# Attended features times W as seven block products instead of eight, with a new order of the work

## The chip, the cores and the metric

One core of a Trainium2 chip. The metric is the device time of one execution in microseconds (us), as the median of several runs; the kernel before takes 2569.77 us (three runs, 2566.48 to 2571.89).

## What is computed

The input is 128 graphs of 128 nodes with 256 features (`x`, fp32), an integer adjacency per graph and a node mask (all ones here). Three graph-attention layers run first, then a gated graph network with three steps; each layer is added to its input.

```python
# layers 0, 1, 2: attention
h = relu(layernorm(x));  Wh = h @ W
e = leaky_relu((Wh @ a1)[:, :, None] + (Wh @ a2)[:, None, :], 0.2)
x = x + elu(softmax(where(adj > 0, e, -9e15)) @ Wh)     # times nodemask in layer 2
# layer 3: gated graph network, three steps i
h = relu(layernorm(x))
m = h @ weight[i];  aggr = einsum('bst,bsd->btd', adj != 0, m)
h = gru_cell(aggr, h, w_ih, w_hh, b_ih, b_hh)
x = x + h
```

## The kernel before, in words

**Groups.** The graphs are worked in 33 groups: two graphs in the first and the last, four in the 31 between (`SIZES`). For each group the function `gat` does the three attention layers and the normalization ahead of layer 3, and `gru` the three recurrent steps. A graph has 128 nodes, so a node is a partition, and a group of four is 512 columns (T).

**Attention of one group and layer** (`attention`). VectorE takes statistics (L519), GpSimd the inverse root (L525, L528), ScalarE normalizes into `xn` (L602), VectorE forms the two scores per graph with a multiply and sum into a scratch tile `scr` (L610). ScalarE and VectorE form the softmax in `em`; its transpose goes by DRAM into `at` (`exchanged`, L552 and after). Then come the two products that matter here. `gathered(k)` (L723) multiplies `xn` by the attention: per half k of the features four matmuls of 128 columns (one per graph) into one bank of PSUM, which ScalarE copies to `ah[:, k]` (L730). `pair(j)` (L742) multiplies these attended features by W: for each of two graphs two matmuls (k = 0, 1) of 256 columns, the stationary side being a 128x128 block of `ah`, the moving side the rows k of W. Two graphs fill one bank `hp`. ScalarE takes the exponential of it (L756) and VectorE adds elu to `x` in two instructions (L758, L760). So a call of four graphs has 16 matmuls of 128 columns and 8 of 256.

**Recurrent step** (`gru`). The aggregation (L991) and the gates (L952, L965, L1047). The gates' products are already in the seven-product form: two 2x2 block matrices are multiplied with seven products of blocks instead of eight, for sums of blocks on both sides (`t13`, `t24` of the state and of the aggregate, L929 and L923 on VectorE; the weights' sums made once by `combinations` on GpSimd, L388), and with copies and additions of partial results in PSUM (L1099, L1103, L1106, L1112; L1015, L1017, L1022 for the new state).

**What sets the order.** No instruction is issued where the code stands. `Plan.add` records each instruction with an engine, a cost in us, a rank and the tiles that it reads, writes and takes. `Plan.issue` then walks through all of them, keeping for each engine a time at which it is free, and issues the ready instruction that can start first, or one within `WINDOW` of it with a lower rank; only ranks within `AHEAD` (`EARLY` at the start, until `UNTIL`) of the lowest open one are looked at. `LAG` is the time it allows between a producer on one engine and a consumer on another. Ranks come from `stage(g, l)` and `start(g, i)`: tables `ATT` and `STARTS` for the first groups, lines of slope 3.0 per group after them. The order on each engine is fixed when the kernel is built; on the chip each engine runs its list in order and waits on semaphores. All DMAs are issued by SP.

**Tiles.** PSUM has eight banks: `gat` 2 (both `ahp` and both `hp`, in turn), `gru` 3, `seed` 2, `tr` 1. `scr` has two buffers, `x` six.

Of the kernel before, what the change touches and what calls it, by code (L numbers as in the profile page):

```python
# [14 lines left out]
P = 128  # L15
# [24 lines left out]
class Plan:  # L40
# [4 lines left out]

    LAG = {"PE": 0.26, "DVE": 0.2, "ACT": 0.2, "POOL": 0.15}
    WINDOW = 0.097
    AHEAD = 4.12
    EARLY = 5.00
    UNTIL = -1.46  # L50

# [12 lines left out]
    def add(self, engine, cost, rank, fn, reads=(), writes=(), after=(), takes=()):  # L64
# [4 lines left out]
        vals = list(dict.fromkeys(v for v, _ in reads + writes))  # L69
        vals += [v for v in dict.fromkeys(takes) if v not in vals]  # L70
        op = Op(engine, cost, rank, fn, vals)
        for v in vals:
# [32 lines left out]
    def lag(self, d, engine, data=True):  # L105
        if d.engine == "SP":
            return d.lands
        return 0.0 if d.engine == engine else self.LAG[d.engine] if data else 0.08

# [79 lines left out]
def kernel(  # L189
# [28 lines left out]
    G = 4  # L218
    FAR = 2
    SIZES = [2] + [G] * ((B - 4) // G) + [2]  # L220
    NG = len(SIZES)
# [60 lines left out]

    SETUPS = [-4.77, -3.63, -3.63, -3.63, -3.63, -3.63, -3.63]
    setting = [0]
# [19 lines left out]

    W, VA = [], []

    def attention_weights(l, w, a):
        rank = [-6.42, -7.21, -4.35][l]
        wt, va = const_val(f"w_{l}", [KD, D]), const_val(f"va_{l}", [2, D])
        first = [-11.17, -10.17, -7.80][l]  # L310
        load(256, first, lambda: nc.sync.dma_start(
# [27 lines left out]
        W.append(wt)  # L339
        VA.append(va)  # L340

    for l, (w, a) in enumerate(((w0, a0), (w1, a1), (w2, a2))):
# [4 lines left out]
    def mask():  # L347
        nm = val(su, "nm", [N], "nm")
        nmp = bank("gat", "nmp")
        load(64, setup_rank(), lambda: nc.sync.dma_start(nm.t[:B], nodemask), writes=[nm])  # L350
        add("PE", 0.11, setup_rank(), lambda: nc.tensor.transpose(nmp.t[:, :B], nm.t[:B], ident[:B, :B]),
            reads=[nm], writes=[nmp])
        add("ACT", act(P), setup_rank(), lambda: nc.scalar.copy(nmT.t, nmp.t[:, :B]),
            reads=[nmp], writes=[nmT])
# [183 lines left out]

    def exchanged(srcs, cut, dst, name, n, rank):

# [10 lines left out]
        def blocks(k):  # L551
            add("DVE", dve(n * P), rank, lambda: nc.vector.transpose(  # L552
                tr.t[:, :, :f].rearrange("p j (k b c) -> p k b j c", k=kd, b=n)[:, k],
                cut(k).rearrange("p b (j r) -> p b j r", j=Q),
            ), reads=[srcs[k]], writes=[(tr, k)], takes=[d, dst])
# [13 lines left out]

    def turned_state(src, k, dst, name, n, rank):  # L570

# [7 lines left out]
        ), reads=[(src, k)], writes=[tr], takes=[d, dst])  # L579
        load(64 * n, rank, lambda: nc.sync.dma_start(d.t.rearrange("b p f -> p b f"), tr.t),  # L580
            reads=[tr], writes=[d])

        def back(j):
            load(16 * n, rank, lambda: nc.sync.dma_start(
                dst.t[j * 32 : (j + 1) * 32, : n * P].rearrange("c (m r) -> c m r", r=32),
# [6 lines left out]
    def attention(g, l, xt, cap):  # L592
# [15 lines left out]
        def score(b, s):  # L608
            scr = val(gw, "scr", [D], f"scr_{name}_{b}_{s}")
            add("DVE", dve(D), rank, lambda: nc.vector.scalar_tensor_tensor(  # L610
# [107 lines left out]

        def gathered(k):
            ps = bank("gat", f"ahp_{name}_{k}")  # L720

            def product(b):
                add("PE", pe(P), rank, lambda: nc.tensor.matmul(  # L723
                    summed(ps, b), xn.t[:, b, k * P : (k + 1) * P], turned_weights(b),
                    start=True, stop=True,
                ), reads=[(xn, b), at], writes=[(ps, b)], takes=[ah])

            for b in range(n):
                product(b)
            add("ACT", act(n * P), rank, lambda: nc.scalar.copy(  # L730
                ah.t[:, k, : n * P], ps.t[:, : n * P]), reads=[ps], writes=[(ah, k)])

        for k in range(KD):
            gathered(k)

        def pair(j):
            hp = bank("gat", f"hp_{name}_{j}")
            t = val(gw, "t", [T], f"t_{name}_{j}")

            def product(b, k):  # L740
                c = 2 * j + b
                add("PE", pe(D), rank, lambda: nc.tensor.matmul(  # L742
                    hp.t[:, b * D : (b + 1) * D], ah.t[:, k, c * P : (c + 1) * P],
                    W[l].t[:, k, :], start=(k == 0), stop=(k == KD - 1),
                ), reads=[(ah, k), W[l]], writes=[hp], takes=[t])

            for b in range(2):
                for k in range(KD):
                    product(b, k)
            parts = [(xt, 2 * j), (xt, 2 * j + 1)]  # L750

            def u():
# [8 lines left out]
                u(), t.t, 1.0, u(), op0=OP.min, op1=OP.add), reads=[t, *parts], writes=parts)  # L761

        for j in range(n // 2):
            pair(j)

    def gat(g):
        b0, n = FIRST[g], SIZES[g]
        rank = stage(g, 0)
        xt = val(grp, "x", [G, D], f"x_{g}", bufs=6, cut=n)
        adj_t = val(grp, "adj", [G, N], f"adj_{g}", dtype=I32, cut=n)  # L770
# [57 lines left out]
    def gru(g, xt, am, hn0, h0):  # L828
# [39 lines left out]
        def flat(h):  # L868

            def part(k):  # L870
                add("DVE", 0.42, start(g, 0) - 1.0, lambda: nc.vector.tensor_copy(
                    cut(h.t[:, k, :TG]), first(k)), reads=[h0], writes=[(h, k)], after=[*after, *begun])
# [4 lines left out]
        def step(i, h):  # L877
# [202 lines left out]
            def mixed(c):  # L1080
# [8 lines left out]
                if FAR <= g < NG - FAR:  # L1089
                    ahead.append(state(f"hn{c}", f"hn_{g}_{i + 1}_{c}"))  # L1090
                    turned_state(hnew, c, ahead[c], f"hn_{g}_{i + 1}_{c}", n_g, quick)

# [38 lines left out]
        def end(h):  # L1131
# [3 lines left out]
            if far:  # L1135
                exchanged(
                    [(h, 0), (h, 1)], lambda k: h.t[:, k, :TG].rearrange("p (b j) -> p b j", b=n_g),
                    o, f"o_{g}", n_g, rank,
                )
# [22 lines left out]

    URGENT = 1.00
    SPAN = 2.25
    HEAD = 5.5
    TAIL = 1.5
# [3 lines left out]
    NNR = 0.25  # L1170
    LEAD = 8.5

    ATT = [
        [-8.90, -4.73, -3.23, -1.30],
        [-7.16, -4.64, -3.85, -2.65],
        [-3.70, -1.92, 1.59, 3.59],
        [-0.38, 1.67, 4.29, 4.81],
        [3.81, 5.72, 6.93, 8.03],
        [7.96, 10.27, 13.26, 12.41],
        [9.50, 11.75, 14.74, 15.00],  # L1180
        [12.46, 14.80, 17.00, 18.00],
        [15.66, 17.97, 20.00, 21.29],
        [18.50, 20.75, 23.00, 24.00],
    ]
    STARTS = [
        [1.68, 2.28, 4.42],
        [3.03, 4.63, 6.47],
        [5.97, 6.79, 10.50],
        [9.00, 11.18, 12.82],
        [12.28, 14.00, 16.00],  # L1190
        [14.67, 16.85, 19.17],
        [17.30, 19.87, 22.34],
        [21.00, 23.00, 25.06],
    ]

    def stage(g, l):

        return ATT[g][l] if g < len(ATT) else 3.0 * g - LEAD + (SPAN * l if l < 3 else HEAD)

    def start(g, i):  # L1200

        return STARTS[g][i] if g < len(STARTS) else 3.0 * g + 2.0 * i

# [44 lines left out]
```

## Time and profile before

| | |
|---|---|
| median of 3 runs | 2569.77 us (2566.48 to 2571.89) |
| the profiled execution | 2566.74 us, its span 2565.0 us |
| mean granted TensorE clock | 0.993 |
| L742, features times W | 1536 records of 128x256, 356.2 us busy |
| L723, attention times features | 1536 records of 128x128, 192.5 us busy |
| L610, scores on VectorE | 732 of 128x256, 270.3 us busy |

The profile has records of what each engine did, with start and duration. PE is a TensorE matmul and PEld the load of its stationary side; both are pipelined, so the time of a matmul is the distance from its start to the next one's. DVE is VectorE, ACT ScalarE, POOL GpSimd, SP the engine that issues the DMAs. "Idle before, releaser" is the time for which an engine stood still ahead of an instruction, and whose end let it go on. The chain follows the work that ended last back through whatever released each step.

### The profile page before, as it was taken

Reading aid. Unit: us, or ns where it says so; the run is one execution under the profiler, and the core shown is the slowest. Engines: PE = TensorE matmul, PEld = TensorE weight load, DVE = VectorE, ACT = ScalarE, POOL = GpSimd, SP = SyncE. Lnnn points to the kernel's source line nnn. Section 1 sums busy time; section 2 is a strip of 40 time slices with the busy share of each in tenths; the row PEclk is TensorE's granted clock in tenths of the full one; section 3 lists DMA queues with packets and bytes.
Section 4 is the critical chain, followed back from the end, with each engine's and each line's share of the span. In section 5 each row is a group of like instructions: output and inputs, shape, how many; then the busy total and the mean of one; then the engine's idle time right before and its main releaser. Section 6 shows DMA issues by size and latency. Waiting matters only on the chain.

```text
span 2565.0 us, 39018 instructions
## 1 busy us (share of the span) xinstructions
PE 2527.7 (99%) x12549; PEld 2098.6 (82%) x12549; DVE 2105.9 (82%) x4955; ACT 1768.5 (69%) x4411; POOL 225.1 (9%) x328
## 2 busy tenths in 40 slices
PE   8799999999999999999999999999999999999998
PEld 5688888888888888888888888888888888888887
DVE  6778888888888888888888888888888888888765
ACT  6777676776766776766776666776666777666554
POOL 2210000000000000000000000000000000000000
PEclk8899999999999999999999999999999999999999
DMA  3113343343343333343334333333334443333320
GB/s 106 46 57 97 87 111 108 95 108 95 106 109 99 107 104 95 108 107 103 105 102 96 109 104 106 104 100 100 107 103 104 107 99 101 101 89 97 75 62 13
DMA packets 503123, 245.75 MB, mean 96 GB/s; under 512 B 280579, under 2 KB 472067, under 8 KB 502918
## 3 DMA queue, kind: packets, MB, share of 16 engines
q1 hardware_dynamic: 502918, 243.25, 35.3%
q8 instruction: 100, 1.64, 0.3%
q14 instruction: 105, 0.86, 0.1%
HBM read 139.28 MB, written 103.87 MB: 95 GB/s over the span
## 4 chain that ended last, share of the span: by engine, by line
PE 95%; DVE 2%; ACT 2%; DMA 1%; issue 0%; SPq 0%; POOL 0%; ACTq 0%; DVEq 0%
PE b L965 19%; PE hp L742 13%; PE e L965 13%; PE ni L1047 13%; PE a L965 13%; PE ahp L723 7%; PE agp L991 6%; PE nn L952 6%; PE nnb L952 5%; ACT em L666 0%; DVE scr L610 0%; ACT em L679 0%; PE hnp L852 0%; DMA at<-d_at 0%; ACT hn L791 0%
## 5 line engine op out<-in xcount | busy, mean ns | idle before, releaser
L742 PE MATMUL hp<-w,ah 128*128 128x256 f32 x1536 | 356.2, 384 | 0.5 <-ACT ah L730 0.5
L1047 PE MATMUL ni<-ag,wc_n 128*128 128x512 f32 (+1 forms) x792 | 352.9, 580 | 0.9 <-DVE ni L1041 0.9
L742 PEld LDWEIGHTS hp<-w,ah 128*128 128x128 f32 x1536 | 286.7, 191 | 61.9 <-ACT ah L730 13.1
L610 DVE SCALAR_TENSOR_TENSOR scr<-xn,va 128x256 f32<-128x256 f32 x732 | 270.3, 418 | 36.1 <-ACT xn L602 35.8
L1047 PEld LDWEIGHTS ni<-ag,wc_n 128*128 128x128 f32 x792 | 147.1, 190 | 125.2 <-issue 104.0
L756 ACT ACTIVATE t<-hp 128x512 f32<-128x512 f32 x192 | 104.6, 595 | 201.3 <-PE hp L742 201.2
L1052 ACT ACTIVATE wn<-ni,bi 128x512 f32<-128x512 f32 (+1 forms) x198 | 133.4, 674 | 157.5 <-PE ni L1047 114.5
L991 PEld LDWEIGHTS agp<-am,hn 128*128 128x128 f32 x1536 | 204.7, 191 | 42.7 <-issue 30.8
L991 PE MATMUL agp<-am,hn 128*128 128x128 f32 x1536 | 208.9, 275 | 3.6 <-ACT ag L999 3.0
L525 POOL TENSOR_SCALAR ve<-st 128x4 f32<-128x4 f32 (+1 forms) x132 | 28.4, 215 | 2087.8 <-DVE st L519 1735.5
L965 PE MATMUL a<-h,whh_rz 128*128 128x256 f32 (+1 forms) x792 | 208.8, 373 | 0.8 <-ACT z L1035 0.5
L723 PEld LDWEIGHTS ahp<-at,xn 128*128 128x128 f32 x1536 | 190.6, 196 | 23.0 <-issue 14.4
L602 ACT ACTIVATE xn<-x,nm,rs 128x256 f32<-128x256 f32 x366 | 201.1, 594 | 3.8 <-DVE nm L531 3.8
L965 PE MATMUL a<-ag,wc_rz 128*128 128x256 f32 (+1 forms) x792 | 199.1, 373 | 0.0
L723 PE MATMUL ahp<-at,xn 128*128 128x128 f32 x1536 | 192.5, 279 | 4.6 <-DMA at<-d_at 2.8
L758 DVE SCALAR_TENSOR_TENSOR x<-hp,x 128x512 f32<-128x512 f32 x192 | 124.0, 685 | 71.0 <-ACT t L756 70.9
L519 DVE BATCH_NORM_STATS2 st<-x 128x6 f32<-128x512 f32 x256 | 170.3, 690 | 2.6 <-DMA x<-in_x_dram 2.5
L649 ACT ACTIVATE em<-er,e 128x128 f32<-128x128 f32 x366 | 164.3, 523 | 2.4 <-DMA er<-de 2.3
L666 ACT ACTIVATE em<-em,nmx 128x128 f32<-128x128 f32 x384 | 149.4, 392 | 11.6 <-DVE nmx L662 11.4
L965 PEld LDWEIGHTS a<-h,whh_rz 128*128 128x128 f32 x792 | 140.9, 191 | 16.9 <-issue 0.7
L965 PEld LDWEIGHTS a<-ag,wc_rz 128*128 128x128 f32 x792 | 141.1, 191 | 15.2 <-issue 0.5
L528 POOL TENSOR_TENSOR rs<-ve,mhalf 128x4 f32<-128x4 f32 (+1 forms) x132 | 144.0, 1091 | 11.0
(158 smaller groups left out, 5541.3 us busy)
## 6 DMA issues: line engine op xcount, KB each, us to landing
d_hn<-tr_hn SPq DMA_DIRECT2D x116, 256.0 KB, 2.4
hn<-d_hn SPq DMA_DIRECT2D x464, 64.0 KB, 2.3
er<-de SPq DMA_DIRECT2D x90, 256.0 KB, 3.9
d_at<-tr_at SPq DMA_DIRECT2D x90, 256.0 KB, 2.2
at<-d_at SPq DMA_DIRECT2D x360, 64.0 KB, 2.0
x<-in_x_dram SPq DMA_DIRECT2D x31, 512.0 KB, 5.0
d_h<-tr_h SPq DMA_DIRECT2D x31, 512.0 KB, 2.7
h<-d_h SPq DMA_DIRECT2D x124, 128.0 KB, 2.7
```

The lines of the kernel that those rows point to most:

```text
L519: add("DVE", dve(T), rank, lambda: nc.vector.bn_stats(st.t[:, b, :].rearrange("p b s -> p (b s)"), xt.t[:, b, :].rearrange("p b d -> p d b ...
L528: add("POOL", 1.04, rank, lambda: nc.gpsimd.tensor_tensor(rs.t, ve.t, mhalf[:, :n], op=OP.pow), reads=[ve], writes=[rs])
L602: add("ACT", 0.45, rank, lambda: nc.scalar.activation(xn.t[:, b, :], xt.t[:, b, :], AF.Relu, bias=nm.t[:, b : b + 1], scale=rs.t[:, b : b ...
L610: add("DVE", dve(D), rank, lambda: nc.vector.scalar_tensor_tensor(scr.t, xn.t[:, b, :], 1.0 if far else rs.t[:, b : b + 1], VA[l].t[:, s, ...
L649: add("ACT", 0.55 if far else 0.42, rank, lambda: nc.scalar.activation(em.t[:, b, :], e2_row(b), AF.Prelu, bias=e.t[:, 0, b : b + 1], alph ...
L666: add("ACT", 0.42, rank, lambda: nc.scalar.activation(em.t[:, b, :], em.t[:, b, :], AF.Exp, bias=nmx.t[:, b : b + 1], accum_out=sm.t[:, b ...
L723: add("PE", pe(P), rank, lambda: nc.tensor.matmul(summed(ps, b), xn.t[:, b, k * P : (k + 1) * P], turned_weights(b), start=True, stop=True ...
L742: add("PE", pe(D), rank, lambda: nc.tensor.matmul(hp.t[:, b * D : (b + 1) * D], ah.t[:, k, c * P : (c + 1) * P], W[l].t[:, k, :], start=(k ...
L952: op = add("PE", pe(H), at, lambda: nc.tensor.matmul(ps.t[:, o : o + H], WHH[1].t[:, blk, :], rhs(), start=starts, stop=True, skip_group_c ...
L965: nc.tensor.matmul(ps.t[:, gate * D : gate * D + H], w[0].t[:, blk, gate * P : (gate + 1) * P], rhs(), start=go, stop=w is not WHH, skip_g ...
L991: nc.tensor.matmul(ps.t[:, b * P : (b + 1) * P], s, am.t[:, b, :], start=True, stop=True)
L1047: add("PE", pe(TG), rank + 0.45 + 0.05 * c, lambda k=k: nc.tensor.matmul(ni[c].t[:, :TG], WC[i][1].t[:, k, c * P : (c + 1) * P], ag.t[:, k ...
```

## The change

1. **Seven block products.** In groups 4 to 31 (`BLOCKED`, full groups) `by_blocks` takes the place of `pair`. `ah` is read as 2x2 blocks (feature half by pair of graphs) and W as 2x2 blocks of 128x128. VectorE forms the sums t1, t3 (one instruction of 512 columns) and t2, t4 (256 each); they lie in tiles that are free by then (`t` and `at`). Each of seven products is two matmuls of 128 columns. ScalarE copies two partial results (256 columns each), VectorE makes two additions of 256 columns out of PSUM and into it. Four sums of blocks of each W are made once on GpSimd into `ws`.
2. **The plan.** A cost for an instruction that reads its own engine's last result (`SELF`), 0.25 more before TensorE (`TO_PE`), lower costs for VectorE and ScalarE, other `LAG`, `WINDOW`, `AHEAD`, `EARLY`, `UNTIL`, and other ranks throughout.
3. **Smaller edits.** `scr` has one buffer instead of two, `x` five instead of six; the two `ahp` halves share a bank where a group has two graphs; the reloads of the turned state get a rank of their own; the matmuls of blocked calls are ordered after those of the first two groups.

The diff, cut to its core:

```diff
-    LAG = {"PE": 0.26, "DVE": 0.2, "ACT": 0.2, "POOL": 0.15}
-    WINDOW = 0.097
-    AHEAD = 4.12
-    EARLY = 5.00
-    UNTIL = -1.46
+    LAG = {"PE": 0.26, "DVE": 0.22, "ACT": 0.24, "POOL": 0.2}
+    SELF = {"DVE": 0.1, "ACT": 0.1, "POOL": 0.05}
+    TO_PE = 0.25
+    WINDOW = 0.03488
+    AHEAD = 5.83122
+    EARLY = 6.44967
+    UNTIL = 2.83338
...
+        if engine == "DVE":
+            cost = max(0.08, cost - 0.08) if cost > 0.3 else cost - 0.02
+        elif engine == "ACT":
+            cost -= 0.1
...
-        return 0.0 if d.engine == engine else self.LAG[d.engine] if data else 0.08
+        if d.engine == engine:
+            return self.SELF.get(engine, 0.0) if data else 0.0
+        return (self.LAG[d.engine] if data else 0.08) + (self.TO_PE if engine == "PE" else 0.0)
...
+    BLOCKED = 4
...
+        def both(i, a, b, op, reads):
+            add("POOL", pool(P), rank + 3.0, lambda: nc.gpsimd.tensor_tensor(
+                ws.t[:, i, :], a(), b(), op=op), reads=reads, writes=[(ws, i)])
+
+        both(1, lambda: low(0), lambda: low(1), OP.add, [wt])
+        both(3, lambda: high(0), lambda: low(0), OP.subtract, [wt])
+        both(2, lambda: ws.t[:, 1, :], lambda: high(0), OP.subtract, [wt, (ws, 1)])
+        both(0, lambda: high(1), lambda: ws.t[:, 2, :], OP.subtract, [wt, (ws, 2)])
...
-    def turned_state(src, k, dst, name, n, rank):
+    def turned_state(src, k, dst, name, n, rank, moved):
...
-        load(64 * n, rank, lambda: nc.sync.dma_start(d.t.rearrange("b p f -> p b f"), tr.t),
+        load(64 * n, moved, lambda: nc.sync.dma_start(d.t.rearrange("b p f -> p b f"), tr.t),
...
-            scr = val(gw, "scr", [D], f"scr_{name}_{b}_{s}")
+            scr = val(gw, "scr", [D], f"scr_{name}_{b}_{s}", bufs=1)
...
+        blocked = n == G and g >= BLOCKED
...
+        def by_blocks():
+            C = T // 2
+            t = [val(gw, "t", [T], f"t_{name}_{j}") for j in range(2)]
+            t13, t24, s7 = t[0], at, t[1]
+            s0, s1 = bank("gat", f"h0_{name}"), bank("gat", f"h1_{name}")
...
+            add("DVE", dve(T), rank, lambda: nc.vector.tensor_sub(
+                pairs(t13), ah.t[:, :, C:], ah.t[:, 0, :].rearrange("p (s t) -> p s t", s=2)),
+                reads=[ah], writes=[(t13, 0), (t13, 1)], takes=t)
+            add("DVE", dve(C), rank, lambda: nc.vector.tensor_sub(
+                pairs(t24)[:, 0], block(1, 1), pairs(t13)[:, 0]),
+                reads=[(ah, 1), (t13, 0)], writes=[(t24, 0)])
+            add("DVE", dve(C), rank, lambda: nc.vector.tensor_sub(
+                pairs(t24)[:, 1], block(1, 0), pairs(t24)[:, 0]),
+                reads=[(ah, 1), (t24, 0)], writes=[(t24, 1)])
...
+            def one(ps, c, blk, what, starts=False):
+
+                lhs, lkey = left[what]
+                rhs, rkey = WS[l][blk]
+                for j in range(2):
+                    add("PE", pe(P), rank, lambda j=j: nc.tensor.matmul(
+                        cols(ps, c)[:, j], lhs()[:, j * P : (j + 1) * P], rhs(),
+                        start=starts and j == 0, stop=True, skip_group_check=True,
+                    ), reads=[lkey, rkey], writes=[ps if starts and j == 0 else (ps, c)],
+                        takes=[s1])
...
+            one(s0, 1, 0, "11", True)
+            one(s0, 0, 6, "t3")
+            add("ACT", act(C), rank, lambda: nc.scalar.copy(cols(s1, 1), cols(s0, 1)),
+                reads=[(s0, 1)], writes=[(s1, 1)])
+            add("ACT", act(C), rank, lambda: nc.scalar.copy(flat(s7), cols(s0, 0)),
+                reads=[(s0, 0)], writes=[s7])
+            one(s1, 1, 5, "t2")
+            one(s0, 1, 1, "21")
+            add("DVE", dve(C), rank, lambda: nc.vector.tensor_add(
+                cols(s0, 0), cols(s1, 1), flat(s7)), reads=[(s1, 1), s7], writes=[(s0, 0)])
+            one(s1, 1, 4, "t1")
+            one(s0, 0, 3, "t4")
+            added(0, s0, t[0])
+            add("DVE", dve(C), rank, lambda: nc.vector.tensor_add(
+                cols(s1, 0), cols(s1, 1), flat(s7)), reads=[(s1, 1), s7], writes=[(s1, 0)])
+            one(s1, 1, 2, "22")
+            added(1, s1, t[1])
...
-        xt = val(grp, "x", [G, D], f"x_{g}", bufs=6, cut=n)
+        xt = val(grp, "x", [G, D], f"x_{g}", bufs=5, cut=n)
...
-    URGENT = 1.00
-    SPAN = 2.25
-    HEAD = 5.5
+    URGENT = 0.58323
...
-    LEAD = 8.5
+    LATE = [-7.44700, -5.59420, -2.72270, -1.01720]
...
-        [-8.90, -4.73, -3.23, -1.30],
+        [-10.17170, -5.78748, -3.71072, -2.46369],
...
-        [1.68, 2.28, 4.42],
-        [3.03, 4.63, 6.47],
+        [-0.69277, 0.65123, 4.09406],
+        [3.87967, 5.58010, 6.79594],
...
-        return ATT[g][l] if g < len(ATT) else 3.0 * g - LEAD + (SPAN * l if l < 3 else HEAD)
+        return ATT[g][l] if g < len(ATT) else 3.0 * g + LATE[l]
```

## The prediction

> **What bounds the kernel now.** I read the page's busy shares and slices first, then the chain, then TensorE by stretches of the span.
>
> ```profile
> span 2565.0 us, 39018 instructions
> ...
> PE 2527.7 (99%) x12549; PEld 2098.6 (82%) x12549; DVE 2105.9 (82%) x4955; ACT 1768.5 (69%) x4411; POOL 225.1 (9%) x328
> ...
> PE 95%; DVE 2%; ACT 2%; DMA 1%; issue 0%; SPq 0%; POOL 0%; ACTq 0%; DVEq 0%
> ```
>
> TensorE is busy all the time and is 95% of the chain that ended last. A busy share alone can hide waiting, so the stretches come next (columns: PE, PEld, DVE, ACT, POOL busy, granted clock, DMA share, GB/s):
>
> ```profile
> 1000.00:1768.50 768.50, 768.50 (x3782) 640.80 (x3781) 653.39 (x1521) 541.18 (x1341) 63.56 (x90) 1.00 0.39 103
> 0.00:200.00 200.00, 172.59 (x906) 138.73 (x907) 148.36 (x437) 143.78 (x403) 41.66 (x66) 0.92 0.24 72
> 200.00:2500.00 2300.00, 2297.10 (x11267) 1909.77 (x11266) 1924.04 (x4443) 1593.81 (x3925) 183.46 (x262) 1.00 0.38 100
> 2500.00:2565.00 65.00, 58.05 (x379) 50.14 (x377) 33.47 (x77) 30.86 (x83) 0.00 (x0) 0.97 0.04 13
> ```
>
> From 200 to 2500 us TensorE idles 2.9 us of 2300 at full clock. Waits are in the first 200 us (27.4 idle, and a clock of 0.92) and the last 65 (7.0). So in the middle only fewer or shorter matmuls shorten the run, provided that no other engine becomes late. How long a matmul holds TensorE is not its "mean ns" (they are pipelined: 384 for 256 columns) but the distance between starts:
>
> ```profile
> 1200.34 1.03 PE L965 MATMUL b<-t13h,whh_rz 128*128 128x256 f32 x4
> 1201.20 1.03 PE L965 MATMUL b<-t13a,wc_rz 128*128 128x256 f32 x4
> ...
> 1206.81 1.95 PE L723 MATMUL ahp<-at,xn 128*128 128x128 f32 x16
> 1208.59 0.61 PE L991 MATMUL agp<-am,hn 128*128 128x128 f32 x4
> 1209.04 0.88 PE L742 MATMUL hp<-w,ah 128*128 128x256 f32 x3
> ```
>
> Four records of 256 columns go by in 0.86 us: 0.2155 each. Twenty of 128 columns go by in 2.23 us (1206.81 to 1209.04): 0.1115 each. The program holds 768 matmuls on L742 and the page 1536 records: each fp32 matmul is two records.
>
> **The change part by part.**
>
> *Fewer columns on TensorE.* In groups 4 to 31 (28 groups, three layers, 84 calls) eight matmuls of 256 columns become fourteen of 128; the changed program as built has 84 x 14 = 1176 matmuls on the new line and 96 left on the old. One call: 16 records x 0.2155 = 3.448 us before, 28 x 0.1115 = 3.122 after, 0.326 saved; 84 x 0.326 = 27.4 us. Other matmuls keep number and width. One check: the chain lists the old sixteen records at 3.52 or 3.53 us, not 3.45, since the third waits some 0.07 us for the second half of `ah`. If the new calls wait for nothing, the saving is 84 x 0.40 = 33 us; I let the new waits cost as much as that one.
>
> *The weights' load.* Each record has its own load. In the 20 narrow records loads too stand 0.1115 us apart, so load and matmul keep step, but a load held up by a semaphore has no wide matmul to hide under. The built order puts 256-column matmuls of the recurrent part between most pairs of products, which makes that room.
>
> A rule that speaks against the change stands in the Trainium skill, "TensorE: Matmul & The Clock Gate", section "Back-to-back issue gap": a stream of load and matmul pairs sustains about 81 ns at 128 columns and 131 at 512, so a column costs 2.5 times as much in the narrow form. As an estimate from that page, narrow columns at even 1.3 times the price of 256-wide ones would turn 27 us gained into some 40 lost. This trace differs: 0.1115 us for 128 columns and 0.2155 for 256 are 0.87 and 0.84 ns a column, 1.03 times, and the measurement decides.
>
> *VectorE.* Per call it gains one subtraction of 512 and two of 256 columns, and two additions of 256 out of PSUM. The nearest rows:
>
> ```profile
> L929 DVE TENSOR_TENSOR t13a<-ag 128x512 f32<-128x512 f32 x93 | 63.0, 678 | 4.3 <-ACT ag L999 4.3
> L1022 DVE TENSOR_TENSOR nn<-nnb,s7n 128x256 f32<-128x256 f32 x93 | 39.9, 429 | 36.5 <-ACT wn L1008 36.2
> L923 DVE TENSOR_TENSOR t24a<-t24a,ag 128x256 f32<-128x256 f32 x93 | 39.5, 424 | 3.1
> ```
>
> 0.68 + 2 x 0.424 + 2 x 0.429 = 2.39 us; pipelined behind another instruction a 256-wide one costs only 0.35 (the scores on L610 start 0.35 apart), so 2.0 is the other end. 84 calls: 168 to 200 us, beside TensorE. A group takes 76.85 us (768.5 / 10) and VectorE is busy 65.3 of it; three calls add 6.0 to 7.2, and the group should shrink to 75.9: 94 to 96% busy, against 85%. Two further edits nearly cancel. The order now keeps apart instructions of which the second reads the first's result: 994 such neighbours in the old order, 311 in the new. Such a neighbour costs 0.46 instead of 0.34 at 256 columns (L923 after L923, 1230.73 to 1231.19). Not all 683 saved ones paid it; at most 683 x 0.12 = 82 us are saved. `scr` has one buffer instead of two, so a score right behind a score waits for it: 374 such places, 45 us if each pays 0.12. Hidden by TensorE, as long as VectorE is not late at a place TensorE waits for.
>
> *New waits on TensorE.* Old calls waited twice (both halves of `ah`); new ones also for the three sums, for both additions, and, through the first addition and the next product, for the two ScalarE copies. Queued behind the waiting matmul is all of TensorE, the next group's recurrent part first. Tightest is the last addition. In the built order (group 18, layer 0) the second t1 product is followed by one t4 product (0.22) and two 256-wide matmuls (0.86), so block 2 starts 1.31 us after that product starts. Needed: 0.28 for the product, 0.43 for the addition, 0.19 for a load, and two handoffs of 0.06 (`ah` ends 1209.37, the load that waited for it starts 1209.43): 1.02. It fits with 0.3 us to spare if VectorE is free. Nothing is charged; the lower bound is the 6 us of the 33 above, the upper one is in the rivals.
>
> *ScalarE, GpSimd, queues.* Two copies of 256 columns a call, 0.27 to 0.38 us each by L1017: 45 to 64 us on an engine at 69%. Twelve 128-wide sums of W on GpSimd at 0.45 (L388) are 5.5 us, once, in a stretch where it is busy 42 of 200; at worst they delay a chain of the start by that. No transfer is added; the reloads of the turned state are ranked earlier on SP, where they wait for their data anyway; one buffer less for `x` lets its load start later, and 5.0 us to landing is small beside a group. Cost 0; without that cover, a late `x` would cost VectorE's statistics a few us per group.
>
> *The start and the end.* All ranks and the plan's constants change. Before the first recurrent matmul the built order has 66 us of matmuls against 64; group 1's recurrent part comes 6 us of matmuls earlier (84 against 90). The 27 us idle there could shrink or grow by a third: 0, with both ends at 10 us.
>
> **Sum.** 2566.74 (the profiled execution, span 2565.0) - 27.4 = 2539.3. That execution is 3 us below the median 2569.77 and inside the runs shown (2566.48 to 2571.89); I forecast **2539**, good for 2527 to 2551: the start's 10 us and the waits' 6, which are unlikely to fall on one side together, taken as 12.
>
> **Rivals.**
>
> *The stalls eat the gain.* If narrow records cost 0.123 instead of 0.1115 (one more load delay of 0.07 at every sixth record), 28 x 0.123 = 3.44 equals 3.45: about 2567. For it: the 0.07 at the old wait, and six waits where there were two. Against: the matmuls put between. Half of it gives 2553.
>
> *VectorE late at the additions: slower.* At 95% busy in program order, an addition may find a 512-wide instruction (0.68) ahead: 0.68 - 0.3 = 0.38 us of TensorE. It decides from 0.326 us per call. One late addition per call and 0.08 at two other waits: 0.54 x 84 = 45.4, so 2566.7 - 27.4 + 45.4 = 2585; both late: 2603. For it: the middle's VectorE share, and additions queued behind sums of other groups. Against: TensorE runs three groups at once, and a stall lets VectorE catch up, so it cannot repeat at each call unless VectorE's total passes TensorE's 75.9 us.
>
> *More than the columns.* A better start order and no waits: 33 + 10 us, about 2523.
>
> **How the numbers follow.** Forecast 0.62, more than that 0.10, gain half eaten 0.08, wholly eaten 0.08, slower 0.12. Faster by over 0.2% (5 us, about what a measurement here can tell from no change): 0.62 + 0.10 + 0.08 = 0.80; same 0.08; slower 0.12. The range leaves out the slower case and most of the largest gain: 2526 to 2568.
>
> **What would show it.** Right: the new line's records 0.112 us apart, some 304 us of matmuls (96 x 0.431 + 1176 x 0.223) on the two lines together, idle TensorE in the middle still a few us, a group in 75.9 us, VectorE near 95%. Wrong: TensorE waiting on VectorE additions in the list of waits (the slower rival), narrow starts over 0.12 apart without a semaphore (load), or a first stretch that ends 10 us later.

## The result, and the profile after

The changed kernel takes **2582.11 us** (median of 4 runs, 2581.33 to 2587.64) against 2568.12 us (4 runs, 2566.37 to 2571.89) for the old one on the same chip: ratio 1.0057, 95% interval 1.0038 to 1.0076. It is 0.6% slower; the forecast was 2539 and faster. The profiled execution is the slowest of the four (2587.64 us, 5.5 above the median), so its waits are some us more than those of a usual execution.

The page of the changed kernel: its span, busy shares and the chain that ended last.

```profile
span 2585.9 us, 42107 instructions
...
PE 2530.0 (98%) x13557; PEld 2103.0 (81%) x13557; DVE 2231.5 (86%) x5375; ACT 1811.5 (70%) x4579; POOL 248.2 (10%) x340
...
PE 40%; DVE 8%; ACT 7%; issue 1%; POOL 1%; DMA 1%; SPq 0%; ACTq 0%; DVEq 0%
```

TensorE's busy time looks as before. The chain doesn't: it had 95% on TensorE and now leaves it in every group through which it can be followed (58% of the span). The stretches of the changed kernel (columns as in the prediction) say where.

```profile
0.00:200.00 200.00, 175.77 (x906) 139.94 (x907) 149.31 (x428) 140.70 (x402) 50.59 (x78) 0.97 0.25 73
200.00:1200.00 1000.00, 981.70 (x5257) 814.95 (x5256) 891.61 (x2129) 712.98 (x1793) 91.34 (x115) 1.00 0.37 100
1300.00:2300.00 1000.00, 997.59 (x5396) 835.67 (x5396) 903.67 (x2178) 728.00 (x1824) 83.74 (x117) 1.00 0.38 103
```

The same two later stretches of the old kernel:

```profile
200.00:1200.00 1000.00, 997.52 (x4904) 829.58 (x4903) 843.78 (x1961) 704.36 (x1739) 81.38 (x117) 1.00 0.38 102
1300.00:2300.00 1000.00, 1000.00 (x4920) 833.88 (x4919) 850.30 (x1978) 704.21 (x1745) 83.59 (x119) 1.00 0.38 102
```

The start is as it was (906 records of TensorE in both). From 200 to 1200 us TensorE now stands idle for 18.3 us; the same stretch of the old kernel has 2.5. VectorE (the third of the engines) is at 89 to 90%, not the 94 to 96% of the forecast. Idle time is only part of a late matmul's price, so I also took, for each record, the distance to the next start less the distance that such a record keeps when nothing is late (0.1117, 0.2157 and 0.429 us by width), and added these up by stretch. They are worked out from the traces, a few records are missing, and so they are good to a few us:

| TensorE time lost, us | 0–200 | 200–1200 | 1200–2400 | end |
|---|---|---|---|---|
| old kernel | 51.3 | 6.1 | 3.3 | 6.0 |
| changed kernel | 51.3 | 36.6 | 16.3 | 9.1 |

46.6 us more in all, of which 43.5 in the middle. The span grew by 20.9; with the 27.4 that fewer columns should have saved, 48.3 had to come from somewhere. These waits have that size.

The list of waits of TensorE in the changed kernel from 200 to 1230 us (total, times, longest):

```profile
PE ahp L755 <- DMA at<-d_at: 5.2, 4, 2.2
PE b L1078 <- DVE c L1225: 2.3, 2, 1.4
PE ni L1160 <- DVE ni L1154: 1.6, 6, 0.4
PE b L1078 <- DVE e L1219: 1.4, 1, 1.4
PE e L1078 <- DVE t13a L1042: 1.3, 2, 0.7
PE h L846 <- ACT t L859: 1.2, 5, 0.2
PE h L846 <- DVE t L822: 0.9, 4, 0.4
PE h L846 <- ACT h L857: 0.8, 2, 0.5
```

In the old kernel no line of this list is above 0.7 us in that stretch. The longest waits are for `at`, the turned attention weights, so for the end of the softmax chain; the next four are in the recurrent part. The new products (L846) come behind them, in three short lines of 2.9 us together.

What such a step looks like, from the chain of the changed kernel in one repeating group (start, length):

```profile
1746.74 0.17 DVE nm L562
1746.93 1.13 ACT xn L633 x3
...
1749.59 0.42 DVE scr L641 x2
1750.01 0.60 DVE h L1183
1750.62 0.34 DVE scr L641 x2
...
1752.77 0.60 DVE h L1186
1753.37 0.61 DVE t L822
1754.03 0.94 PE h L846 x6
```

The scores of one group's attention (L641) stand in VectorE's list ahead of four updates of another group's state and of the first block sum (L822). Whatever delays the scores delays all of it, and TensorE waits at the end.

### The profile page after: what moved, and what is told of

The parts are those of the page before. It is cut to its first block, busy times and chain, and to the rows that moved or that the text cites. A ratio compares the mean times of both kernels' runs of the same rounds, so it can differ in the third digit from the quotient of the medians.

```text
span 2585.9 us, 42107 instructions
## 1 busy us (share of the span) xinstructions
PE 2530.0 (98%) x13557; PEld 2103.0 (81%) x13557; DVE 2231.5 (86%) x5375; ACT 1811.5 (70%) x4579; POOL 248.2 (10%) x340
## 4 chain that ended last, share of the span: by engine, by line
PE 40%; DVE 8%; ACT 7%; issue 1%; POOL 1%; DMA 1%; SPq 0%; ACTq 0%; DVEq 0%
PE b L1078 8%; PE a L1078 6%; PE ni L1160 5%; PE e L1078 5%; PE h L846 5%; PE nn L1065 3%; PE ahp L755 2%; PE agp L1104 2%; PE nnb L1065 2%; ACT xn L633 2%; ACT r L1148 1%; ACT em L710 1%; POOL rs L559 1%; DVE x L785 1%; ACT z L1148 1%
## 5 line engine op out<-in xcount | busy, mean ns | idle before, releaser
L1160 PE MATMUL ni<-ag,wc_n 128*128 128x512 f32 (+1 forms) x792 | 362.2, 584 | 5.5 <-DVE ni L1154 3.8
L641 DVE SCALAR_TENSOR_TENSOR scr<-xn,va 128x256 f32<-128x256 f32 x732 | 307.8, 421 | 44.0 <-ACT xn L633 22.7
L556 POOL TENSOR_SCALAR ve<-st 128x4 f32<-128x4 f32 (+1 forms) x132 | 41.9, 318 | 2035.0 <-DVE st L550 1983.4
L1160 PEld LDWEIGHTS ni<-ag,wc_n 128*128 128x128 f32 x792 | 139.3, 190 | 116.8 <-issue 94.6
L755 PE MATMUL ahp<-at,xn 128*128 128x128 f32 x1536 | 199.9, 280 | 6.9 <-DMA at<-d_at 5.7
L680 ACT ACTIVATE em<-er,e 128x128 f32<-128x128 f32 x366 | 172.1, 524 | 9.6 <-DMA er<-de 9.6
L550 DVE BATCH_NORM_STATS2 st<-x 128x6 f32<-128x512 f32 x256 | 172.4, 692 | 2.8 <-DMA x<-in_x_dram 2.6
L765 ACT COPY ah<-ahp 128x512 f32<-128x512 f32 (+1 forms) x198 | 112.0, 573 | 81.5 <-PE ahp L755 74.9
L1078 PEld LDWEIGHTS a<-h,whh_rz 128*128 128x128 f32 x792 | 138.1, 191 | 14.1 <-issue 0.8
L783 ACT ACTIVATE t<-h 128x512 f32<-128x512 f32 x168 | 100.1, 596 | 67.5 <-PE h L846 54.1
L1154 DVE SCALAR_TENSOR_TENSOR ni<-r,wn 128x512 f32<-128x512 f32 (+1 forms) x198 | 127.1, 676 | 12.9 <-ACT z L1148 7.8
L710 ACT ACTIVATE em<-em,ri 128x128 f32<-128x128 f32 x384 | 129.9, 399 | 7.9 <-DVE ri L704 4.2
```

The source lines that it names most:

```text
L550: add("DVE", dve(T), rank, lambda: nc.vector.bn_stats(st.t[:, b, :].rearrange("p b s -> p (b s)"), xt.t[:, b, :].rearrange("p b d -> p d b ...
L680: add("ACT", 0.55 if far else 0.42, rank, lambda: nc.scalar.activation(em.t[:, b, :], e2_row(b), AF.Prelu, bias=e.t[:, 0, b : b + 1], alph ...
L710: add("ACT", 0.39, rank, lambda: nc.scalar.mul(em.t[:, b, :], em.t[:, b, :], ri.t[:, b : b + 1]), reads=[(em, b), ri], writes=[(em, b)])
L755: op = add("PE", pe(P), rank, lambda: nc.tensor.matmul(summed(ps, o + b), xn.t[:, b, k * P : (k + 1) * P], turned_weights(b), start=first ...
L1078: nc.tensor.matmul(ps.t[:, gate * D : gate * D + H], w[0].t[:, blk, gate * P : (gate + 1) * P], rhs(), start=go, stop=w is not WHH, skip_g ...
L1160: add("PE", pe(TG), rank + 0.45 + 0.05 * c, lambda k=k: nc.tensor.matmul(ni[c].t[:, :TG], WC[i][1].t[:, k, c * P : (c + 1) * P], ag.t[:, k ...
```

## The experiments

Three theories. **Load:** the five VectorE instructions that each blocked call adds leave VectorE too little room. **Order:** the new plan's order makes TensorE wait, whatever the products. And, formed on the way, **buffer:** the single scratch tile of the scores, one line of the change, makes scores late in a chain that this order leaves no slack. Times of the old kernel beside the runs were 2568 us in each comparison.

**Eight products in the new plan.**

```diff
-    BLOCKED = 4
+    BLOCKED = 99
```

> The changed kernel with the new plan and ranks, but no blocked call: all calls use the eight products of 256 columns. Theory A (VectorE has more work per group than the order gives it time for, so TensorE waits for late VectorE results): the 27 us of columns come back, VectorE's share of the middle falls from 90% to about 85%, and TensorE's waits between 200 and 2400 us fall from about 45 us to about 10: some 2573 us. Theory B (the new order itself makes the waits, whatever the products are): the waits stay and the columns come back: some 2605 us or more.

Measured: 2612.81 us, ratio 1.0171 (1.0156 to 1.0187), as theory B had it. The windows of this run from 200 to 1200 and from 1300 to 2300 us:

```profile
200.00:1200.00 1000.00, 983.66 (x4799) 810.58 (x4798) 827.14 (x1941) 688.45 (x1713) 87.61 (x117) 1.00 0.37 99
1300.00:2300.00 1000.00, 987.07 (x4814) 814.13 (x4813) 824.40 (x1935) 689.96 (x1708) 86.00 (x115) 1.00 0.37 101
```

Without one block product and with VectorE at 82 to 83%, below the old kernel's share, TensorE stands idle 16.3 and 12.9 us. So the waits do not need the products or their load. And under the same constants and due times the products are worth 2612.8 - 2582.1 = 30.7 us (the two kernels have two orders, since the plan arranges other instructions).

**The elu's sums made light.**

```diff
-                u(), hp.t, 0.0, u(), op0=OP.max, op1=OP.add), reads=[hp, *parts], writes=parts, after=[power])
+                u()[:, :16], hp.t[:, :16], 0.0, u()[:, :16], op0=OP.max, op1=OP.add), reads=[hp, *parts], writes=parts, after=[power])
```

and the same in the second sum.

> The changed kernel with the same order on every engine, but the two VectorE instructions that add elu to x work on 16 of 512 columns (the other columns of x are left without it): VectorE loses about 2 us a call, as much as the block products add, and no path of the block products' own sums gets shorter. Theory A (VectorE's load): TensorE's waits in the middle fall from about 45 us to under 15, time near 2550 us. Theory B (the order) and theory C (narrow weight loads that come late cost TensorE twice, with nothing to do with VectorE's load): within 5 us of 2582.

Measured: 2567.91 us, 1.0001 (0.9991 to 1.0010): 14.2 us back for 167.6 us less on VectorE (2231.5 to 2063.9). That lies between the two expectations: VectorE's load has a part in the waits, and not the larger one.

**Blocks under the old constants and due times.**

```diff
-    LAG = {"PE": 0.26, "DVE": 0.22, "ACT": 0.24, "POOL": 0.2}
+    LAG = {"PE": 0.26, "DVE": 0.2, "ACT": 0.2, "POOL": 0.15}
...
-    WINDOW = 0.03488
+    WINDOW = 0.097
...
-    SETUPS = [-3.37484, -1.49751, -3.36328, -3.55562, -1.02629, -3.79206, -3.59543]
+    SETUPS = [-4.77, -3.63, -3.63, -3.63, -3.63, -3.63, -3.63]
```

> The block products with the old plan: old constants, old ranks, one scr buffer and five x buffers as in the changed kernel. Theory A: VectorE is as loaded, so TensorE waits at least as much as with the new plan: 2580 to 2620 us. Theory B: the old order had 10 us of waits in the middle, and they stay few: some 2545 us.

Measured: 2752.55 us, 1.0716 (1.0700 to 1.0732); TensorE idles 62 us between 200 and 1200. Both expectations missed by far. Due times fit the instructions that they were chosen for; the same block products cost 170 us more under these.

**Blocks from group 14 on.**

```diff
-    BLOCKED = 4
+    BLOCKED = 14
```

> The changed kernel with block products from group 14 on, where the order repeats from group to group; groups 4 to 13, whose ranks come from the tables, use the eight products. 30 calls go back to wide products, which costs 30 x 0.326 = 10 us of columns. Theory A: the 30 us of extra waits between 200 and 1230 us go with the VectorE work, time near 2562 us. Theory B: they stay, time near 2592 us.

Measured: 2589.15 us, 1.0076 (1.0060 to 1.0093): 7.0 slower than the changed kernel for 30 calls without blocks (30 x 0.326 = 9.8 by the columns). That is near theory B. The products gain in that region too, and it waits with eight nearly as with seven (TensorE idle for 15.2 us from 200 to 1200, and 18.3).

**Two scratch tiles.** Two tiles of 16 bits take the room of one of 32.

```diff
-            scr = val(gw, "scr", [D], f"scr_{name}_{b}_{s}", bufs=1)
+            scr = plan.val(gw, "scr", 1, lambda: gw.tile(
+                [P, D], mybir.dt.bfloat16, tag="scr", name=f"scr_{name}_{b}_{s}", bufs=2))
```

> The changed kernel in the same order, with the scores' scratch tile kept in 16 bits so that two of them fit again (the product that each score writes there is read by nobody; its sum is kept in 32 bits as before). Only the reuse of one buffer goes. One-buffer theory: a score behind a score steps 0.379 us apart with one buffer and 0.346 with two, 24 scores per group, so VectorE has 0.8 us less per group (1.1 with the waits at the ends), some 30 us over the run; the measured exchange rate is 14 us for the 195 us of VectorE that light elu sums took away, so about 2 us come back: 2575 to 2582. Rival (the single buffer delays the scores where TensorE waits for what follows them, as in the page's waits for the turned weights and the row sums): most of the difference to the old kernel comes back, 2562 to 2570.

Measured: **2554.53 us**, 0.9947 (0.9933 to 0.9962). 27.6 us back from this line, the order unchanged: the rival, and more than it asked for. Two neighbouring scores in the changed kernel, then in this one (start, length):

```profile
1748.04 0.42 DVE L641 SCALAR_TENSOR_TENSOR scr<-xn,va 128x256 f32<-128x256 f32 x1
1748.39 0.08 DVE L641 DVE_READ_ACCUMULATOR scr<-xn,va 128x1 f32 x1
1748.57 0.42 DVE L641 SCALAR_TENSOR_TENSOR scr<-xn,va 128x256 f32<-128x256 f32 x1
```

```profile
1720.47 0.42 DVE L642 SCALAR_TENSOR_TENSOR scr<-xn,va 128x256 bf16<-128x256 f32 x1
1720.82 0.08 DVE L642 DVE_READ_ACCUMULATOR scr<-xn,va 128x1 f32 x1
1720.82 0.42 DVE L642 SCALAR_TENSOR_TENSOR scr<-xn,va 128x256 bf16<-128x256 f32 x1
```

Each score lasts 0.42 in both. With two tiles the next one starts 0.35 later, while the last one's record still runs; with one it starts 0.53 later (0.47 and 0.53 in turn along this row of scores, so the 0.379 of the expectation was too small). The groups of rows say the sum (busy, mean ns, idle before): the changed kernel, then this one.

```profile
L641 DVE SCALAR_TENSOR_TENSOR scr<-xn,va 128x256 f32<-128x256 f32 x732 | 307.8, 421 | 44.0 <-ACT xn L633 22.7 <-ACT z L1148 0.5
```

```profile
L642 DVE SCALAR_TENSOR_TENSOR scr<-xn,va 128x256 bf16<-128x256 f32 x732 | 282.0, 420 | 25.0 <-ACT xn L633 24.3
```

25.8 us of busy time and 19.0 of idle time: 44.8 us of VectorE. My 45 was right in size. Of them 27.6 ended in the time. TensorE with two tiles:

```profile
200.00:1200.00 1000.00, 990.40 (x5377) 831.95 (x5376) 897.52 (x2169) 723.21 (x1814) 93.95 (x117) 1.00 0.38 101
1300.00:2300.00 1000.00, 1000.00 (x5437) 842.89 (x5436) 901.80 (x2193) 735.56 (x1847) 83.45 (x117) 1.00 0.38 104
```

Its lost time fell from 36.6 to 18.7 us between 200 and 1200 and from 16.3 to 7.3 after it, and the chain is back on TensorE in the repeating groups:

```profile
PE 63%; DVE 2%; ACT 1%; DMA 1%; issue 0%; POOL 0%; SPq 0%; DVEq 0%; ACTq 0%
```

**Width or number?**

```diff
-                [P, D], mybir.dt.bfloat16, tag="scr", name=f"scr_{name}_{b}_{s}", bufs=2))
+                [P, D], mybir.dt.bfloat16, tag="scr", name=f"scr_{name}_{b}_{s}", bufs=1))
```

> The changed kernel in the same order with the scores' scratch tile in 16 bits, but one of it as in the changed kernel. It splits the 27.6 us that the pair of 16-bit tiles brought (2582.1 to 2554.5). Buffer theory: the width of the scratch is nothing, the second buffer is all: 2577 to 2585, scores' busy time 308 us as in the changed kernel. Rival (a 16-bit result is simply written faster, the second buffer is nothing): 2552 to 2560 and 282 us of scores.

Measured: 2582.51 us, 1.0055 (1.0040 to 1.0070), scores 308.6 us busy. It is the number of tiles.

**One scratch tile in the old kernel.**

```diff
-            scr = val(gw, "scr", [D], f"scr_{name}_{b}_{s}")
+            scr = plan.val(gw, "scr", 2, lambda: gw.tile(
+                [P, D], FT, tag="scr", name=f"scr_{name}_{b}_{s}", bufs=1))
```

> The old kernel in its own order, with one scores' scratch tile for two and nothing else changed. Theory that the single buffer costs the time of the scores wherever TensorE is short of room: the scores get 0.033 us each slower here too (270 us to some 308), but the old order leaves TensorE only some 9 us of waits in the middle and VectorE 85%, so less than half of 27.6 shows: 2570 to 2582. Rival (the buffer's cost goes straight into the time): 2592 to 2600. Rival (the old order hides it all): 2566 to 2570.

Measured: 2577.51 us, 1.0034 (1.0021 to 1.0047), +9.2 us. Its first 200 us and the middle:

```profile
0.00:200.00 200.00, 170.56 (x860) 135.75 (x861) 143.16 (x409) 134.57 (x377) 40.94 (x65) 0.92 0.22 66
200.00:1200.00 1000.00, 997.25 (x4893) 828.48 (x4892) 857.85 (x1969) 706.89 (x1745) 82.33 (x116) 1.00 0.38 102
1300.00:2300.00 1000.00, 1000.00 (x4920) 833.88 (x4919) 866.40 (x1980) 704.28 (x1743) 82.75 (x117) 1.00 0.38 103
```

The scores of the old kernel, then of this run:

```profile
L610 DVE SCALAR_TENSOR_TENSOR scr<-xn,va 128x256 f32<-128x256 f32 x732 | 270.3, 418 | 36.1 <-ACT xn L602 35.8
L611 DVE SCALAR_TENSOR_TENSOR scr<-xn,va 128x256 f32<-128x256 f32 x732 | 308.3, 421 | 61.9 <-ACT xn L602 35.8
```

VectorE pays more than in the new order (38.0 us busy and 25.8 idle: 63.8), and the middle hardly shows it: TensorE 997.25 and 1000.00 busy, as in the old kernel. Nearly all of the 9 us are in the first 200, by whose end 46 records of TensorE fewer have run (860 for 906). So my reading "beside TensorE" holds for the old order after its start, and for that order alone.

**Light scores: the place or the amount?**

```diff
-                scr.t, xn.t[:, b, :], 1.0 if far else rs.t[:, b : b + 1], VA[l].t[:, s, :],
+                scr.t[:, :16], xn.t[:, b, :16], 1.0 if far else rs.t[:, b : b + 1], VA[l].t[:, s, :16],
```

> The changed kernel in the same order, one 32-bit scratch tile, with each score on 16 columns for 256 (most of the scores' sums is left out). That takes about 0.25 us from each of 768 scores, some 190 us of VectorE, as much as the light elu sums did (195 us, worth 14 us). Place theory (the scores stand in the chain row, softmax, turned weights, products, whose end TensorE waits for): 30 to 45 us, 2537 to 2552, so several times what the same relief brought at the elu. Amount theory (VectorE's room is what counts): 14 us again, 2564 to 2572.

Measured: **2539.02 us**, 0.9887 (0.9873 to 0.9902). The busy line of the light elu sums, then of the light scores:

```profile
PE 2515.5 (98%) x13557; PEld 2100.4 (82%) x13557; DVE 2063.9 (81%) x5375; ACT 1815.3 (71%) x4579; POOL 235.7 (9%) x340
```

```profile
PE 2499.9 (99%) x13557; PEld 2105.3 (83%) x13557; DVE 2062.7 (81%) x5375; ACT 1808.0 (71%) x4579; POOL 243.4 (10%) x340
```

The same VectorE busy time to 1.2 us, the same order, and 28.9 us between them: 14.2 us gained at the elu, 43.1 at the scores. So the relief of the scores is worth more, and the time lies in the place theory's range. How much of that is the place alone stays open: some of the 43.1 is the same late reuse of the tile, now short, and less the 27.6 of the two tiles only 15.5 are left, about what the elu sums brought. The clearer case for the place is the run with two tiles: 44.8 us less of VectorE at the scores gave 27.6, 167.6 less at the elu 14.2.

**Eight products with two tiles.** The edits of the first and the fifth experiment together.

> The new plan and code with eight products in every group, and the pair of 16-bit scratch tiles in place of the one tile of 32 bits. Against 2612.8 with one tile: if the single buffer is most of what the new order loses, 2580 to 2590 and the order itself is left with some 12 to 22 us over the old kernel. If the buffer only costs with the block products' VectorE load beside it: 2600 to 2612.

Measured: 2581.39 us, 1.0052 (1.0035 to 1.0069), inside the first of the two ranges. Now the change adds up step by step: the new order with eight products and two tiles costs 2581.4 - 2568.1 = 13.3 us, seven products bring 2581.4 - 2554.5 = 26.9, and the single tile costs 2582.1 - 2554.5 = 27.6. (With one tile the products bring 30.7, and with eight products the tile costs 31.4.) The 13.3 us hold all else that was changed, the five buffers of `x` too. Those are hardly at fault: VectorE's statistics stood idle 2.6 us for `x` in the whole run before (L519) and 2.8 after (L550).

**Other orders.** The first run moves the plan's constants. They were not drawn blindly: of many such draws this one lost least on TensorE when every instruction was given the duration that the changed kernel's profile shows.

```diff
-    SELF = {"DVE": 0.1, "ACT": 0.1, "POOL": 0.05}
-    TO_PE = 0.25
+    SELF = {"DVE": 0.0750, "ACT": 0.0174, "POOL": 0.05}
+    TO_PE = 0.2037
...
-    AHEAD = 5.83122
+    AHEAD = 5.65468
...
-        rank = [-5.79151, -6.16570, -5.91413][l]
+        rank = [-5.79151, -6.16570, -5.46167][l]
```

> The changed kernel with the same instructions, put in another order: the plan's lags, its window, two costs and eight of its due times are moved a little (costs by up to 6 ns, lags by up to 0.08 us, due times by up to 0.9). Order theory: the waits belong to the order and not to the products or to VectorE's load, so another order of the same instructions with the same VectorE load can do without a good part of them: 2555 to 2570, and VectorE's busy time unchanged within 5 us. Load theory: the same load gives the same waits, 2578 to 2586.

Measured: 2567.51 us, 0.9999 (0.9989 to 1.0008), VectorE 2231.5 us busy, to the tenth what the changed kernel has. The order theory held: 14.6 us are the order's, at the same load.

```diff
-            add("ACT", 0.45, rank, lambda: nc.scalar.activation(
+            add("ACT", 0.594, rank, lambda: nc.scalar.activation(
...
-            add("ACT", 0.42, rank, lambda: nc.scalar.activation(
+            add("ACT", 0.487, rank, lambda: nc.scalar.activation(
...
```

> The changed kernel with two of the plan's ScalarE costs put right by the profile: the scaled copies into xn and hn (planned at 0.35, stepping 0.493 on the chip) and the softmax exponential (0.32 against 0.387). Nothing else is touched; the order that comes out is another. Theory that the new plan's costs are too low and so its order has no slack: with truer costs there are fewer waits, 2555 to 2572. Rival (any new input only draws another order, and the due times fit the costs they were chosen with): no better than now, 2580 to 2630.

Measured: 2602.64 us, 1.0136 (1.0120 to 1.0151). My theory that the plan's low costs are the cause falls: two truer costs with the old due times gave a worse order.

**Both, and what is left.** Another order with two tiles known to the plan (its constants moved as above, by other amounts):

> The changed kernel with the pair of 16-bit scratch tiles, known to the plan too, and with the plan's lags, window, costs and due times moved a little, as in the run with another order. Order theory (the order and the buffer are two separate losses, 14.6 and 27.6 us): most of both comes back, 2537 to 2549. Rival (both take the same waits away): 2550 to 2556, as the pair alone.

Measured: **2550.10 us**, 0.9930 (0.9915 to 0.9945), the fastest complete version here: 18.2 us below the old kernel in that comparison. It is 4.4 us below the two tiles alone, where another order with one tile had brought 14.6. So order and tile seem to take away mostly the same waits; the two orders are not the same one, so the size of the overlap isn't shown.

Two tiles and the light elu sums, in the changed kernel's order:

> The changed kernel in the same order with the pair of 16-bit scratch tiles, and the elu's two VectorE sums on 16 columns for 512 (left out but for a strip), which takes some 195 us off VectorE. What still lies between 2554.5 and the forecast of 2539: if it is VectorE's load, the 14 us that the light sums brought with one buffer come again, 2538 to 2543. If the pair has already taken away the waits that VectorE's load made, 2548 to 2554 and the rest is the order's.

Measured: 2544.02 us, 0.9909 (0.9893 to 0.9926): 10.5 us less than with two tiles alone, between the two expectations. About that much of the 15.5 us that lie above the forecast goes with VectorE's load.

Light elu sums, light exponentials and light scores together:

> The changed kernel in the same order, with the elu's two VectorE sums, its exponential on ScalarE and the scores each on 16 columns for 512: the additions, the exponentials and the scores are left out but for a strip. VectorE and ScalarE do much less between the same instructions of TensorE. Order theory (TensorE meets chains of other engines that the order leaves too late, engines loaded or not): the light sums alone gave 2568 with some 40 us of waits left; with the scores and exponentials short too the chains are shorter and 2550 to 2562 is expected, waits still above those of the old kernel's 9 us in the middle. Load theory (the waits are other engines' backlog): they go entirely, and what is left is TensorE's own work, 2582 less 45, 2535 to 2545.

Measured: 2528.40 us, 0.9852 (0.9837 to 0.9867), below what both theories gave. After 1200 us TensorE loses 1.2 us to waits there (16.3 in the changed kernel), and the start is some 12 us shorter too. So in the repeating groups this order holds TensorE up only through the other engines' work that was made light here. The time itself can't be set against the forecast, since much of the work is left out.

## Why the prediction was wrong, point by point

**Columns: right.** 27.4 forecast, 26.9 measured with two tiles (30.7 with one). TensorE's own work says the same: 2352 narrow records at 0.1117 us in place of 1344 wide ones at 0.2157 are 27.2 us less. Narrow records keep 0.11 us each in the changed kernel when nothing is late, with their loads:

```profile
1644.78 0.39 PE L846 MATMUL h<-w,ah 128*128 128x128 f32 x2
1645.00 0.39 PE L846 MATMUL h<-ws,at 128*128 128x128 f32 x2
1645.22 0.39 PE L846 MATMUL h<-ws,t 128*128 128x128 f32 x2
```

Two records in 0.22 us, and 26.9 us gained: the rival that the stalls eat the gain is out, and so is the estimate from the Trainium skill's rule in "TensorE: Matmul & The Clock Gate", section "Back-to-back issue gap".

**VectorE's added work: too high.** By their durations the five new groups of rows are 57.4, 35.1, 35.0, 35.2 and 35.8 us, 198.5 together, the upper end. Much of that overlaps with neighbours: with two tiles VectorE is busy for 2207.0 us with the block products and 2058.6 without, so they cost 148.4, below my 168. The same 2058.6 lies 47.3 us below the old kernel's 2105.9, which fits the smaller number of own-result neighbours (82 was the most I allowed); no run parts it from the rest of the new order. So the share is 90% and not 94 to 96%.

**The scratch tile: this step failed.** It was priced at 45 us of VectorE and measured at 44.8, and then charged nothing: "Hidden by TensorE, as long as VectorE is not late at a place TensorE waits for." VectorE is late there. I took the cover from the old profile (85% busy, TensorE never waiting), and the old order does give it: one tile in the old kernel leaves the middle untouched. The changed kernel has another order. I had its list of instructions and asked it only about one addition of one call, never how much room it leaves behind the scores.

**The new order charged at 0 ± 10 us, at the start alone: failed too, by 13.3 us.** "All ranks and the plan's constants change" stood under start and end. The start of the changed kernel lost no more than before (51.3 us in both); the middle lost 43.5 us more, tile included. With eight products and two tiles, so without either of the other terms, TensorE still stands idle for 14.1 us between 200 and 2400, the old kernel's for 2.9.

**New waits, allowed some 6 us: too low with one tile, about right with two.** I count, as in the table above, what a record comes late, and put it to the record that is late. From 200 to 2400 us the products of L742 lost 3.9 us in the old kernel; those of L846 lose 19.2 in the changed one, its largest group (a good third of all that is lost there), and 9.2 with two tiles. The wait at 1754.03 in the chain above is one of them. They are not what made the kernel slower: with eight products and two tiles TensorE loses as much in the middle as with seven (some 29 us and some 27), at other lines.

**The slower rival named nearly the right time (2585) by luck, and the wrong place.** It needed late additions behind VectorE at 95%, once per call. Its condition did not come (90%); the loads on L846 stood idle for 6.9 and 5.3 us before the two additions in the whole run, 38 times in 168; and with no block addition at all the kernel is slower still (2612.8). The loss comes in chains that were there before, those behind the scores above all, as two tiles and light scores show.

**The sum.** 2568.1 + 13.3 - 26.9 + 27.6 = 2582.1; it closes by construction, since each term is the difference of two runs. Without the last term it is 2554.5; the forecast of 2539 also lacks the order's 13.3. A group takes 76.67 us in the changed kernel (1465.43 to 2002.10, seven groups), 76.17 with two tiles, 75.77 with light scores; 75.9 was forecast.

## What to carry to other kernels

Where a change makes the whole order anew, the old profile's "off the critical path" doesn't hold for the new order: every edit that lengthens another engine's chain, above all a buffer given up to make room, has to be priced once as hidden and once as exposed, and the range has to hold both. Look for such an edit beside the headline: here one buffer fewer cost 27.6 us, all of the 26.9 that the products gained. And ask where in the engine's list a delay lies before asking how much it is: 168 us off VectorE were worth 14 us at the elu's sums, and 45 us off it at the scores' tile were worth 28.

## What the runs showed of the hardware that was not expected

A VectorE instruction that must wait for the one before it loses more than a look at its duration tells: scores of 0.42 us start 0.35 apart with two scratch tiles and 0.47 to 0.53 with one. The Trainium skill, "VectorE: DVE Perf Modes", section "The DRAIN you can't avoid", holds that a semaphore after each operation "costs nothing extra here", as measured there for copies. The case isn't the same, since here the next score waits for the last one's tile; for these scores the wait costs 0.12 to 0.18 us each, and the measurement decides.

A late narrow matmul costs more than its wait. TensorE's rows of the changed kernel at the wait shown above, with the load that waited:

```profile
1753.56 0.38 PE L846 MATMUL h<-w,ah 128*128 128x128 f32 x2
...
1754.02 0.30 PEld L846 LDWEIGHTS h<-ws,t 128*128 128x128 f32 x2 [0.27 <-DVE t L822]
1754.03 0.49 PE L846 MATMUL h<-ws,t 128*128 128x128 f32 x2
...
1754.35 0.39 PE L846 MATMUL h<-w,ah 128*128 128x128 f32 x2
```

The pair at 1754.03 was due at 1753.78 (0.22 after 1753.56): 0.25 us late. Then it takes 0.32 us for its two records instead of 0.22: its first matmul's record starts with its load (1754.02), where records that come in time start 0.11 us after theirs (load 1645.12, matmul 1645.22). All 20 pairs on this line that came over 0.15 us late behind another narrow record took 0.32 us. That 0.10 is busy time to the profile, so the idle column alone shows too little, and the table of starts is needed.
